# A two-layer graph network: adjacency blocks issued by ScalarE's queue, and four W loads ahead of the residual rows

## The chip, the cores and the metric

The kernel runs on one core of a Trainium2 chip. The time is the device time of that core in microseconds (us). Three runs of the kernel before gave 3094.37, 3098.48 and 3099.01 us; their median is 3098.48 us. The engines are called as in the profile: PE multiplies matrices, DVE does vector work, ACT does activations and copies, POOL (GpSimd) does sums and issues stores, and SP only issues DMAs. Every engine takes its own instructions in order. "SPq" is an instruction that issues a DMA from SP's queue, "ACTq" one from ACT's.

## The reference

There are 2708 rows of 1024 features, and an adjacency matrix of 2708 x 2708 integers, 0 or 1. Two layers follow each other, each with a layer norm ahead and a residual sum behind it:

```python
# layer 0
h = jnp.maximum(_layernorm(x), 0.0)
f = h @ Wf + bf;  g = h @ Wg + bg
e = jax.nn.relu(f @ g.T)
attention = softmax(jnp.where(adj > 0, e, NEG), axis=1)
x = x + attention @ (h @ W + bW)
# layer 1
h = jnp.maximum(_layernorm(x), 0.0)
hw = h @ W1
e = leaky_relu(hw @ a1 + (hw @ a2).T, 0.2)
attention = softmax(jnp.where(adj > 0, e, NEG), axis=1)
x = x + relu(attention @ hw)
```

The scores of layer 0 are a full product of 2708 x 2708 numbers; those of layer 1 are a sum of a column and a row.

## The kernel before

**Panels and pairs.** The scores are made transposed, in five panels p of query columns (576, 576, 532, 512 and 512 wide, `width[p]`). The rows (keys) go in ten pairs q of 128-row tiles, and a rest called LEFT (index 10). Products are taken in Strassen's manner: seven products, named M1 to M7, in the place of eight, and sums by DVE and POOL between them. So `sx`, `sy` and `sz` in the profile are three accumulators of the scores, which take M1 and M2, M5 and M3, M6 and M7 and M4; `px`, `py`, `pz` and `pv` are those of a projection with W.

**Order of the work.** A program for a panel is `project_q` (makes the right operands B), `scores(p, B)`, then softmax and `aggregate` (attention times h), then `project` (times W). `project_q` of the next panel, or in the end `project` of an earlier one, stands between scores and aggregation, so that DVE's softmax lies beside products. The last such projection of the code's layer 0 goes by pairs of tiles (`by_pair`), with the residual rows `x_res` added in `finish0`. It is the one that the change touches, and it runs from about 2085 to 2143 us, ahead of layer 1's aggregation.

**Scores.** For each pair q, `scores` calls `fetch(q + 2)`: the adjacency block of the pair after next, in one stream buffer `adj_i` and, for panels 0 to 2, a slot `adj_t` for the columns over 512. `square_rows` does it by groups of 32 partitions, so a block takes 4 issues and its tail another 4 (8 and 8 for LEFT). Each row's piece is 64 integers of 4 bytes (32 for LEFT). Then come the products M1, M6, M5, M2, M7, M3, and M4, the last one delayed into the next pair. Their left operands `As` come from `hs_d` in DRAM, two products to a tile: M1 with M6, M5 with M2, M7 with M3, and M4 alone. Between the products DVE adds the accumulators into the scores, turns the block of pair q + 1 into a mask (`convert`, `turn`), and does small tasks from a list (`behind`).

**In the first panel** the rows of x are still being read while the scores start: layer norm (`x<-x,rs` on ACT, with its root `rs<-mv`), the transposes `hsT` on PE and ACT, and the stores of `hs_d` for the later pairs run beside the products of the first ones (`make_until(q + 2)`).

**Buffers and queues.** `stream` is a pool of 12 buffers in rotation, for As, adj_i, W (`w`), the left operands of the aggregation (`hc`) and others. A W for one product takes two of them. `load` (L137 to 139) issues from SP and keeps the program's order on the queue. Stores, and the bias that is added into `x_res` in DRAM-to-buffer transfers with an accumulate, are issued by POOL.

**W in the last projection.** `project` loads W for the first two products in `order` (M1 and M5 when by pairs), then calls `start_of`, which for each of the panel's four tiles issues a mask (`maskl`) and the residual rows `x_res` in eight pieces (32 loads in all). W of the other products is loaded where it is used, `ws.pop(m) if m in ws else load_W(l, m)`. By pairs, the whole W is read once for each of the two pairs.

Of the kernel before, what the change touches and what calls it, by code (L numbers as in the profile page):

```python
# [20 lines left out]
B32 = 32  # L21
# [36 lines left out]
def kernel(  # L58
# [19 lines left out]
    nc = InOrder(tc)  # L78
# [46 lines left out]
    def slot(name, shape=(P, WX), dt=FP):  # L125
        return slots.tile(list(shape), dt, tag="slot", name=name)

    def stream(name, shape=(P, D), dt=FP):
        return strm.tile(list(shape), dt, tag="strm", name=name)

    def in_16(o, i):

        n = o.shape[0]
        k = n // 16 * 16
        return [(o, i)] if n in (k, 1) or not k or i.shape[0] != n else [(o[:k], i[:k]), (o[k:], i[k:])]

    def load(o, i):  # L137
        for a, b in in_16(o, i):
            tc.keep_in_program_order(nc.sync.dma_start(a, b))

    def store(o, i):
        for a, b in in_16(o, i):
            nc.gpsimd.dma_start(a, b)  # L143
# [81 lines left out]
    def row_to_all(v, t):  # L225
        load(t, bass.AP(tensor=v.tensor, offset=v.offset, ap=[[0, P], [1, D]]))
        return t
# [38 lines left out]
    def row_on_all(o, row, p, by=load):  # L266
        by(o[:, :width[p]], row[0:1, :width[p]].to_broadcast([P, width[p]]))
# [10 lines left out]
    def load_rows_of(t, o, a):  # L278

        for e in range(2):  # L280
            if t == TINY:
                nc.gpsimd.memset(o[e], 0.0)
            for ps, r in places[t]:
                load(o[e][ps], a[r:r + ps.stop - ps.start, e * W:(e + 1) * W])
# [248 lines left out]
    def fetch_wg(b):  # L533
        return [load_rows(wg, 4 * b + i, "wg") for i in range(4)]
# [60 lines left out]
    ws = fetch_wg(0)  # L595
# [8 lines left out]
    for a in range(NC):  # L604
# [5 lines left out]
        if a == NH:  # L610
# [4 lines left out]
            ws = fetch_wg(1)  # L615
# [150 lines left out]
    def mask_maker(p):  # L766

        r0, w = base[p], width[p]
        NG, NB = P // B32, W // B32
        tail = -(-(w - W) // B32)  # L770
        raw, neg = {}, {}

        def columns(q):

            if q < LEFT:
                return [[start_of_tile(t) + P * g for g in range(NG)] for t in pairs[q]]
            return [[base[g // 2] + W + g % 2 * B32 for g in range(NG)], [base[2] + W] * NG]

        def fetch(q):
            a = stream("adj_i", (P, NB, 2, B32), I32)  # L780
            b = slot("adj_t", (P, tail, 2, B32), I32) if tail else None
            raw[q] = a, b
            c0, c1 = columns(q)

            def square_rows(t, blocks, g, k, r, j, n):
                load(t[B32 * g:B32 * (g + 1), :, k] if k is not None else
                     t[B32 * g:B32 * (g + 1)].rearrange("p b k c -> p b (k c)"),
                     adj[r:r + blocks * B32, j:j + n].rearrange("(b r) j -> r b j", r=B32))
            for t, blocks, r in ((a, NB, r0), (b, tail, r0 + W)):
                for g in range(NG if t is not None else 0):  # L790
                    if q < LEFT:
                        square_rows(t, blocks, g, None, r, c0[g], 2 * B32)
                    else:
                        for k, c in enumerate((c0, c1)):
                            square_rows(t, blocks, g, k, r, c[g], B32)

        def convert(q):
            a, b = raw.pop(q)
            neg[q] = []
            for t, blocks in ((a, NB), (b, tail)):  # L800
                if t is not None:
                    m = slot("nm", (P, 2, blocks, B32), BF)
                    nc.vector.tensor_scalar(m, t.rearrange("p b k c -> p k b c"), 0.0, -BIG, op0=OP.is_le, op1=OP.mult)
                    neg[q].append(m)

        def turn(q, k):
            if k == 0:
                mk_sb[p, q] = slot("mask", (P, 2, WX), BF)
            mk = mk_sb[p, q]
            m = neg[q]  # L810
            nc.vector.transpose(mk[:, k, :W].rearrange("p (s g r) -> p g s r", s=F, g=NG),
                                m[0][:, k].rearrange("p (g s) c -> p g s c", g=NG))
            if tail:
                nc.vector.transpose(mk[:, k, W:W + tail * B32].rearrange("p (b r) -> p b r", r=B32), m[1][:, k])
            if k == 1:
                neg.pop(q)
                store(mk_d[p][:, q], mk[:, :, :w])

        return fetch, convert, turn
# [373 lines left out]
    def load_W(l, m):  # L1193
        ts = [stream("w", (P, 2, W)) for _ in range(2)]
        for g, t in enumerate(ts):
            if m in (M1, M2, M3):
                r, c = (2 * g * P, 0) if m == M1 else ((2 * g + NH) * P, 0 if m == M2 else W)
                load(t, w_in[l][r:r + 2 * P, c:c + W].rearrange("(k p) o -> p k o", p=P))
            else:
                load(t, wt_d[l][:, {M5: 0, M6: 1, M7: 2, M4: 3}[m], 2 * g:2 * g + 2, :])  # L1200
        return [ts[k // 2][:, k % 2] for k in range(NH)]

    def project(l, p, G, finish, then={}, by_pair=False, rate=2.0):
# [10 lines left out]
        start_of, join, finish = finish  # L1214

        order = (M1, M5, M2, M6, M7, M3, M4) if by_pair else (M1, M2, M5, M6, M3, M7, M4)
        ws = {m: load_W(l, m) for m in order[:2]}
        start_of([t for g in todo for t in g[:2]] + ([other] if other else []))
        def left_of(ta, tb, one, two):
            (a11, a12), (a21, a22) = one, two  # L1220
# [33 lines left out]
        for j, group in enumerate([[t] for t in todo] if by_pair else [todo]):  # L1254
            acc, tmp = {}, {}
            left = lefts.pop(j)
            for m in order:
# [4 lines left out]
                for i, (ta, tb, _, _) in enumerate(group):  # L1262
# [9 lines left out]
                    o = {M3: M6, M7: M5, M4: M1}.get(m)  # L1272
# [396 lines left out]
    for p in range(NP):  # L1669
# [8 lines left out]
        if p + 1 < NP:  # L1678
            B = project_q(p + 1, hooks)
        else:  # L1680
            nc.hold = ("vector",)
            project(0, p - 1, G.pop(p - 1), finish0(p - 1), hooks)
            nc.hold = ()
            scores_before()
# [15 lines left out]
        if p < NP - 2:  # L1700
            project(0, p, G.pop(p), finish0(p), {M1: lambda p=p: first_masks(p + 1, 0),
                                                 M5: lambda p=p: first_masks(p + 1, 1),
                                                 M7: lambda p=p: first_masks(p + 1, 2)})
    flush()
    project(0, NP - 1, G.pop(NP - 1), finish0(NP - 1), by_pair=True, rate=0.0)


# [129 lines left out]
```

## Time and profile before

| | us |
|---|---|
| median of three runs | 3098.48 |
| the profiled execution | 3099.78 |
| its span in the profile | 3098.0 |
| PE busy | 3002.8 |
| DVE busy | 2070.7 |
| ACT busy | 463.2 |
| POOL busy | 506.3 |

The granted clock of PE was 0.989 of full speed over the span. In a timeline, a line has the start, the busy time, the engine, the source line, the operation with out and in, and a count of like instructions in a row; in brackets at its end, the idle time ahead of it and what ended that idle time. A line of SPq is a row of DMA issues: its time is the time of the issuing alone, and includes waits between the issues of the row. The chain of waits is followed back from the last instruction; a line "DMA name" in it is the time from an issue to the landing. In the table of windows the columns are the window, its length, then busy time (and count) of PE, PE's weight loads, DVE, ACT and POOL, then the granted clock, the DMA engines' share and GB/s.

The groups that matter for the change, as the profile has them: the scores' products take 293.5 us for `sz`, 199.6 for `sx` and 199.3 for `sy`; before `sx` PE stood idle for 6.4 us in the whole span, before `sz` for 11.8, before `sy` for 2.3.

### The profile page before, as it was taken

To read this page: it belongs to the slowest core of one execution; us is meant where nothing else is said; L and a number is where in the kernel's file an instruction comes from. 1 tells how busy PE (TensorE), PEld (TensorE's weight loads), DVE (VectorE), ACT (ScalarE), POOL (GpSimd) and SP (SyncE) were. 2 spreads that over 40 slices of the span, in tenths; PEclk is the share of its full clock that TensorE was granted. 3 is DMA by queue.
4 is the path that set the end of the run, shared out by engine and by line. 5 is a ranking of instruction groups with operands and counts; after the bars stand their busy time and mean duration, and the time that the engine had idled before them with its cause. 6 is when DMAs were issued, how large, how long until landed. Compare 5 with 4: busy or idle time off the path is not lost.

```text
span 3098.0 us, 41680 instructions
## 1 busy us (share of the span) xinstructions
PE 3002.8 (97%) x14630; PEld 2298.1 (74%) x14630; DVE 2070.7 (67%) x4615; ACT 463.2 (15%) x817; POOL 506.3 (16%) x786
## 2 busy tenths in 40 slices
PE   8998999899999999999999999997999999999998
PEld 4576777657877588885888886783777969879694
DVE  5767693776651596716975277766968768887853
ACT  3420020010110101101011001301222121212200
POOL 1421101310011110214101001141202010020202
PEclk9999999999999999999999999998999999999999
DMA  6999967998565796758967577789667868888896
GB/s 225 291 257 254 301 247 253 309 274 229 178 238 153 217 260 223 244 158 241 278 199 255 164 217 234 237 266 350 229 216 249 274 202 296 287 269 294 264 297 246
DMA packets 448577, 764.70 MB, mean 247 GB/s; under 512 B 175776, under 2 KB 262592, under 8 KB 448368
## 3 DMA queue, kind: packets, MB, share of 16 engines
q1 hardware_dynamic: 393008, 598.31, 62.0%
q0 software_dynamic: 55360, 163.73, 16.4%
q8 instruction: 116, 1.90, 0.3%
q14 instruction: 93, 0.76, 0.1%
HBM read 627.95 MB, written 133.91 MB: 246 GB/s over the span
## 4 chain that ended last, share of the span: by engine, by line
PE 71%; DVE 11%; DMA 7%; issue 7%; SPq 2%; POOL 1%; ACT 1%; POOLq 0%; DVEq 0%; ACTq 0%
PE sz L1378 6%; PE gx L661 6%; PE gy L661 6%; PE gz L661 5%; PE gz L1067 5%; PE pz L1267 4%; PE sx L1378 4%; PE sy L1378 4%; PE px L1267 4%; PE py L1267 3%; PE gx L1067 3%; PE gy L1067 3%; PE M_ps L574 3%; PE qz L661 2%; PE qx L661 2%
## 5 line engine op out<-in xcount | busy, mean ns | idle before, releaser
L1378 PE MATMUL sz<-B,As 128*128 128x288 f32 (+2 forms) x1200 | 293.5, 394 | 11.8 <-DVE st L45 8.8
L1378 PEld LDWEIGHTS sz<-B,As 128*128 128x128 f32 x1200 | 227.8, 191 | 61.8 <-DVE st L45 12.7
L1378 PE MATMUL sx<-B,As 128*128 128x288 f32 (+2 forms) x800 | 199.6, 392 | 6.4 <-DMA As<-hs_d 4.4
L1378 PE MATMUL sy<-B,As 128*128 128x288 f32 (+2 forms) x800 | 199.3, 392 | 2.3 <-DMA As<-hs_d 2.3
L661 PE MATMUL gz<-Sa,hc 128*128 128x288 f32 (+2 forms) x800 | 189.2, 397 | 6.3 <-DMA hc<-hg_d 6.3
L661 PEld LDWEIGHTS gz<-Sa,hc 128*128 128x128 f32 x800 | 153.8, 193 | 40.1 <-DMA hc<-hg_d 6.8
L1378 PEld LDWEIGHTS sx<-B,As 128*128 128x128 f32 x800 | 151.3, 190 | 40.1 <-DMA As<-hs_d 3.7
L1378 PEld LDWEIGHTS sy<-B,As 128*128 128x128 f32 x800 | 152.0, 190 | 33.4 <-issue 2.7
L1067 PE MATMUL gz<-quarter,hc 128*128 128x128 f32 (+2 forms) x1344 | 168.8, 279 | 3.8 <-DVE gT L45 3.7
L143 POOL DMA_DIRECT2D out_dram<-x_res x180 | 89.0, 501 | 482.1 <-DVE x_res L45 474.7
L1067 PEld LDWEIGHTS gz<-quarter,hc 128*128 128x128 f32 x1344 | 160.6, 191 | 5.1 <-DVE gT L45 4.6
L1267 PE MATMUL px<-w,gT 128*128 128x512 f32 x320 | 143.9, 602 | 7.5 <-DMA w<-in_L_gnn_W_dram 6.0
L1267 PE MATMUL pz<-w,ps 128*128 128x512 f32 x320 | 142.1, 594 | 0.8 <-DVE pt L45 0.8
L1267 PE MATMUL py<-w,ps 128*128 128x512 f32 x320 | 142.0, 593 | 0.0
L143 POOL DMA_DIRECT2D mk_d<-mask x55 | 35.8, 652 | 534.8 <-DVE mask L45 528.1
L1267 PEld LDWEIGHTS px<-w,gT 128*128 128x128 f32 x320 | 60.9, 193 | 80.9 <-issue 74.7
L1267 PEld LDWEIGHTS pz<-w,ps 128*128 128x128 f32 x320 | 60.2, 190 | 77.1 <-issue 70.7
L1267 PEld LDWEIGHTS py<-w,ps 128*128 128x128 f32 x320 | 60.5, 190 | 75.8 <-issue 73.9
L574 PE MATMUL M_ps<-wgT,wfT 128*128 128x512 f32 x256 | 113.5, 600 | 1.6 <-ACT hsT L45 1.6
L661 PE MATMUL gy<-T,hc 128*128 128x288 f32 (+2 forms) x480 | 111.6, 394 | 0.0
L977 POOL TENSOR_TENSOR gT<-gT,rr 128x2304 f32<-128x2304 f32 (+5 forms) x12 | 44.4, 3700 | 382.4 <-DVE rr L45 179.8
L661 PEld LDWEIGHTS gy<-T,hc 128*128 128x128 f32 x480 | 91.2, 190 | 19.5
(377 smaller groups left out, 5803.6 us busy)
## 6 DMA issues: line engine op xcount, KB each, us to landing
hc<-hg_d SPq DMA_DIRECT2D x175, 512.0 KB
As<-hs_d SPq DMA_DIRECT2D x150, 512.0 KB
hc<-hr_d SPq DMA_DIRECT2D x119, 512.0 KB
hc<-hs_d SPq DMA_DIRECT2D x112, 512.0 KB
w<-wt_d SPq DMA_DIRECT2D x96, 512.0 KB
w<-in_L_gnn_W_dram SPq DMA_DIRECT2D x72, 512.0 KB
md<-md_d SPq DMA_DIRECT2D x56, 512.0 KB
adj_i<-in_adj_dram SPq DMA_DIRECT2D x200, 128.0 KB
```

What stands on the lines that cost most here:

```text
L143: nc.gpsimd.dma_start(a, b)
L574: nc.tensor.matmul(ps, wfT[a][c // NH][:, c % NH, :], wgT[b][c], start=(c == 0), stop=(c == NC - 1))
L661: nc.tensor.matmul(ps[d], left(m, k, d), right(m, k), start=(start and k == 0), stop=(k == K - 1), skip_group_check=True)
L977: nc.gpsimd.tensor_tensor(of(e, s), of(e, s), by(s, k), OP.mult)
L1067: nc.tensor.matmul(ps[:, d], lhs[:, d * P:(d + 1) * P], inner_right(m, n, k), start=(start and k == 0 and d == 0), stop=(k == NK - 1), ski ...
L1267: nc.tensor.matmul(ps, left[i][m][:, k, :], w_[k], start=(start and k == 0), stop=(k == NH - 1), skip_group_check=True)
L1378: nc.tensor.matmul(ps[:n, :h], lefts[q][:, i % 2, c, :n], B[m][c // 2][:, c % 2, :h], start=(start and c == 0), stop=(c == NH - 1), skip_g ...
```

## The change

First, `load` takes the engine that issues, SP by default. `square_rows` gives ACT for every block from pair 2 on, so that only the first two blocks of a panel stay on SP. This holds for all five panels: in panels 0 to 2, 80 issues each, in panels 3 and 4, 40 each, 320 in all. The blocks, their buffers and their order among themselves stay as they were. Second, `project` loads W for the first four products (M1, M5, M2, M6) ahead of `start_of` when it goes by pairs and `l` is 0, in place of two.

```diff
-    def load(o, i):
+    def load(o, i, by=nc.sync):
         for a, b in in_16(o, i):
-            tc.keep_in_program_order(nc.sync.dma_start(a, b))
+            tc.keep_in_program_order(by.dma_start(a, b))
...
             def square_rows(t, blocks, g, k, r, j, n):
                 load(t[B32 * g:B32 * (g + 1), :, k] if k is not None else
                      t[B32 * g:B32 * (g + 1)].rearrange("p b k c -> p b (k c)"),
-                     adj[r:r + blocks * B32, j:j + n].rearrange("(b r) j -> r b j", r=B32))
+                     adj[r:r + blocks * B32, j:j + n].rearrange("(b r) j -> r b j", r=B32),
+                     nc.scalar if q > 1 else nc.sync)
...
         order = (M1, M5, M2, M6, M7, M3, M4) if by_pair else (M1, M2, M5, M6, M3, M7, M4)
-        ws = {m: load_W(l, m) for m in order[:2]}
+        ws = {m: load_W(l, m) for m in order[:4 if by_pair and l == 0 else 2]}
         start_of([t for g in todo for t in g[:2]] + ([other] if other else []))
```

## The prediction

> **What bounds the kernel now.** I read the page's busy table first, then the chain of waits, then the DMA issues, and then TensorE's timeline, looking for bracketed idle times in the stages that the change touches.
>
> ```profile
> PE 3002.8 (97%) x14630; PEld 2298.1 (74%) x14630; DVE 2070.7 (67%) x4615; ACT 463.2 (15%) x817; POOL 506.3 (16%) x786
> ...
> PE 71%; DVE 11%; DMA 7%; issue 7%; SPq 2%; POOL 1%; ACT 1%; POOLq 0%; DVEq 0%; ACTq 0%
> ...
> As<-hs_d SPq DMA_DIRECT2D x150, 512.0 KB
> ...
> adj_i<-in_adj_dram SPq DMA_DIRECT2D x200, 128.0 KB
> ```
>
> TensorE (PE) works for 3002.8 of 3098.0 us: 95.2 us of idle time is all that better feeding could ever give, and a delay counts in full as soon as it reaches PE. ACT is busy for 15%, so issuing there looks free; but its queue is in order, and what stands behind an issue matters, not its share. As (the left operands of the scores, 512 KB each) and the adjacency blocks both come from SP's queue. In the first panel's scores (about 218 to 375 us) PE waits for As:
>
> ```profile
> 224.24 2.11 PE L1378 MATMUL sy<-B,As 128*128 128x288 f32 x8
> ...
> 246.00 3.63 PE L1378 MATMUL sz<-B,As 128*128 128x288 f32 x8 [2.38 <-DMA As<-hs_d]
> ...
> 253.94 2.21 PE L1378 MATMUL sx<-B,As 128*128 128x288 f32 x8 [2.13 <-DMA As<-hs_d]
> ...
> 278.58 2.18 PE L1378 MATMUL sy<-B,As 128*128 128x288 f32 x8 [2.25 <-DMA As<-hs_d]
> ```
>
> With 0.70 at 270.24 and 1.57 at 288.14 these five waits make 9.03 us: the whole that part A can win there. SP's timeline shows what As stands behind:
>
> ```profile
> 198.25 2.23 SPq L139 DMA_DIRECT2D adj_i<-in_adj_dram  x4
> ...
> 203.00 11.70 SPq L139 DMA_DIRECT2D x<-in_x_dram  x16
> 214.80 0.94 SPq L139 DMA_DIRECT2D As<-hs_d  x2
> 215.91 3.74 SPq L139 DMA_DIRECT2D adj_i<-in_adj_dram  x4
> ...
> 271.78 11.47 SPq L139 DMA_DIRECT2D adj_t<-in_adj_dram  x4
> 284.24 2.17 SPq L139 DMA_DIRECT2D As<-hs_d  x4
> ```
>
> The chain of waits gives the reason at 271.78: an issue waits for the landing of an earlier adjacency block.
>
> ```profile
> 262.31 6.14 DMA adj_t<-in_adj_dram
> ...
> 268.51 15.65 DMA adj_i<-in_adj_dram
> ```
>
> **What the skill says.** The Trainium skill, "DMA: Bandwidth & Descriptors", section "Issuing engines are not separate DMA queues", says that DMAs of SP, ACT and POOL run on the same 16 engines, and that a second issuer saves only the issuing time. The trace agrees as far as it goes: at 200 to 300 us the DMA share is 0.91 to 1.04, so there is no idle transfer capacity for a second queue to use. [...] "Perfetto Trace Analysis", section "DMA Instruction — HWDGE (DVE, Sync)", says that the record of an issue leaves out the transfer; I therefore take landings from the chain (3.85 us the shortest adjacency landing, at 1457.50; As 3.77 and 6.98).
>
> **What the built programs add.** In both, every DMA issued by SP or ACT signals one of eight shared semaphores, and each waits until the DMA before it on its semaphore has landed. The order across the two queues is thus fixed: at most eight are under way, and an SP load can wait for a block that ACT has not issued yet. The move does not free As from adj; it makes SP's loads depend on how far ACT is.
>
> **Part A, first scores.** Removed from SP: 80 issues (8 for each of eight row pairs, 16 for the rest). Added to ACT: the same 80. ACT's timeline shows where they come to stand:
>
> ```profile
> 220.13 1.52 ACT L45 ACTIVATE x<-x,rs 128x512 f32<-128x512 f32 x2 [1.02 <-DVE rs L45]
> ...
> 238.00 1.52 ACT L45 ACTIVATE x<-x,rs 128x512 f32<-128x512 f32 x2 [0.48 <-DVE rs L45]
> 242.18 0.30 ACT L45 ACTIVATE rs<-mv,eps 128x1 f32<-128x1 f32 x1 [2.66 <-DVE mv L45]
> ```
>
> (1) Pair 2's blocks, which SP issued at 198.25 to 202.4, follow the x copies of 220.13 on ACT, so most start at 221.7 or later. In SP's queue the second to ninth of the 16 x loads wait for these blocks' semaphores, and behind the x loads stands the As tile for M5 and M2 of pair 0 (214.80 before). First landing 221.7 + 3.85 = 225.6. The x loads took 11.70 us for 16; at half to two thirds of that As is issued at 231 to 233 and lands 3.8 to 7 later, 235 to 240. PE needs it at 224.24: a stall of 11 to 15, of which I take 12. Nothing hides it, since PE has no other product ready.
> (2) After such a pause PE is slower: after the pauses of 8.33 and 3.85 us before 2160 the granted clock was 0.70.
>
> ```profile
> 2150.00:2175.00 25.00, 19.51 (x70) 14.34 (x71) 25.00 (x65) 9.26 (x17) 2.90 (x4) 0.70 0.78 243
> ```
>
> The first gx group there took 21.60 us, the next 19.40; I take +1.5 (0 to 2).
> (3) Pair 3's eight issues follow the x copies of 238.00 and stand ahead of the root of 242.18 and the hsT copies of 244.38; the sixth waits until the first has landed. DVE's reciprocal after that root is in DVE's in-order queue, behind it the addition that PE's M7 waits for. +3 to +8; I take +4.
> (4) The five waits of 9.03: PE comes 12 us later, so its As tiles are there, but the transfers that SP couldn't start are also late, in a stage whose transfers are full. I take -7 (-9 to 0).
> Sum of the first scores: 12 + 1.5 + 4 - 7 = +10.5.
>
> **Part A, later scores.** Panel 1: pair 2's blocks go from 630.73 on SP to after 661.12 on ACT; As for M1 and M6 of pair 1 then waits for their landing near 669, lands 674 to 676, needed at 672.83: +2 to +3. Pair 3's follow the x_res copies of 678.84, and As of pair 2 comes about 3 us late, partly beside waits for DVE that are there anyway. I take +3.5 (0 to 6). Panels 2 and 3: the same step leaves As of pair 1 at 1099 (needed 1099.4) and 1465 (needed 1464.2): +1.5 together (0 to 4). Panel 4: ACT is free and PE doesn't wait for loads: 0.
>
> **Part B.** Before, only W for M1 and M5 stands ahead of 32 x_res loads and four masks; M2's comes after them:
>
> ```profile
> 2080.83 7.90 SPq L139 DMA_DIRECT2D x_res<-in_x_dram  x8
> 2088.77 1.82 SPq L139 DMA_DIRECT2D w<-in_L_gnn_W_dram  x2
> ...
> 2098.14 6.29 PE L1267 MATMUL px<-w,gT 128*128 128x512 f32 x8 [5.96 <-DMA w<-in_L_gnn_W_dram]
> ```
>
> Moved up: four issues, 2 MB. They go, but need four stream buffers that the aggregation frees between 2060.3 and 2068.6, so x_res starts near 2069 instead of 2058.97. The 5.96 go, perhaps 0.78 at the next product as well: -6.7 at most. Next late is W for M7 (issued at 2090.69 before), behind the same x_res loads at about 2099, 1 to 5 us; and DVE's first sum with x_res (2092.21), which already waited 2.45 us for the bias. I take -3 (-6 to +2).
>
> **Sum.** 10.5 + 3.5 + 1.5 - 3 = +12.5. The profiled execution has 3099.78 us (span 3098.0, 1.78 outside it), the median of the three runs is 3098.48; on the median this is 3111.0.
>
> **Rivals.**
> - As freed (faster). If ACT's blocks are issued early enough, before about 220, the M5 tile isn't late; As no longer stands behind 11 us of adjacency issues, all 9.03 go and part B gives 3: 3098.5 - 12 = 3086.5. For it: the five brackets and 271.78. Against it: the shared semaphores, and ACT's x copies at 220.13.
> - Given back (no change). The stall of 12 comes, with its 1.5, but scores that start later find all their loads there (-9) and part B gives -5: about 3098. For it: most loads after 250 wait for buffers that PE frees. Against it: the full DMA engines.
> - ACT blocked everywhere (heavier). The upper ends: 15 + 1.5 + 8 - 7, then 6, 4 and 2: +29.5, 3128. For it: each ACT block can wait for its own landings. Against it: ACT has little to do after 260.55.
>
> **How the numbers follow.** Forecast 0.50, faster 0.20, given back 0.18, heavier 0.12. Range 3088 to 3126: it leaves out about half of the faster case and half of the heavier, 0.16. Without the faster case the forecast's own range is 3104 to 3120. What a measurement can tell from no change is 0.2%, 6.2 us: faster 0.21 (the faster case and an edge of "given back"), same 0.19, slower 0.60.
>
> **What would show it.** In the changed kernel's trace: x loads on SP pausing from 203 to about 225; one wait of 10 us or more for As at the first sy products; less than 3 us of As waits from 246 to 290; ACT's roots behind adjacency issues; As waits of 2 to 3 us near 672 on top of the shift; no W wait at px, a smaller one at the M7 pz. I am wrong if SP's x loads go on at 204, or if the M5 tile lands before PE asks for it.

## The result, and the profile after

The changed kernel took 3117.49 us (median of six runs, 3114.05 to 3122.06); the kernel before, run beside it, 3097.6 us. The ratio is 1.0065, with a 95% interval of 1.0052 to 1.0078: about 20 us slower, where +12.5 was forecast. The profiled execution took 3114.05 us, the shortest of the six, so that what is found in it (+14.3 against the first profile of before) falls short of the whole.

The first lines of the two parts of the page, engines and chain of waits, of the changed kernel:

```profile
PE 3002.5 (96%) x14630; PEld 2299.3 (74%) x14630; DVE 2070.3 (67%) x4615; ACT 463.1 (15%) x817; POOL 506.1 (16%) x786
...
PE 69%; DVE 9%; issue 7%; DMA 5%; POOL 1%; ACT 1%; SPq 0%; ACTq 0%; POOLq 0%; DVEq 0%
```

PE is busy for the same time (3002.5 against 3002.8 us), so in sum what was lost is time in which PE waits: 109.7 us of the span of 3112.2, against 95.2. SP's timeline at the start of the first scores, the place where the prediction put the loss:

```profile
193.40 0.38 SPq L139 DMA_DIRECT2D As<-hs_d  x1
194.88 28.92 SPq L139 DMA_DIRECT2D x<-in_x_dram  x16
223.90 1.33 SPq L139 DMA_DIRECT2D As<-hs_d  x3
```

The 16 x loads that took 11.70 us before take 28.92, and As stands behind them. The view of waits, for SP from 190 to 225 us (total, times, longest), names what they wait for:

```profile
SPq L139 <- DMA adj_i<-in_adj_dram: 21.3, 3, 20.1
```

One wait of 20.1 us is for an adjacency block, which is no longer in SP's queue. ACT's timeline has it:

```profile
211.06 0.29 ACT L45 ACTIVATE rs<-mv,eps 128x1 f32<-128x1 f32 x1 [7.15 <-DVE mv L45]
211.17 0.38 ACTq L45 DMA_DIRECT2D adj_i<-in_adj_dram  x1
...
212.48 0.81 ACT L45 ACTIVATE x<-x,rs 128x512 f32<-128x512 f32 x1 [1.02 <-DVE rs L45]
...
214.07 1.99 ACTq L45 DMA_DIRECT2D adj_t<-in_adj_dram  x4
```

The first of the block's eight issues goes out at 211.17, right behind a root of the layer norm for which ACT had waited 7.15 us (for DVE's `mv`), and SP's next x load at 215.27. PE's timeline, lines with an idle time ahead of them and one that follows such a line:

```profile
227.88 4.18 PE L1379 MATMUL sy<-B,As 128*128 128x288 f32 x8 [11.13 <-DMA As<-hs_d]
231.85 3.14 PE L1379 MATMUL sx<-B,As 128*128 128x288 f32 x8
...
258.28 3.65 PE L1379 MATMUL sz<-B,As 128*128 128x288 f32 x8 [7.96 <-DVE st L45]
...
290.79 3.04 PE L1379 MATMUL sy<-B,As 128*128 128x288 f32 x8 [3.38 <-DMA As<-hs_d]
```

There are two new waits, 11.13 us for As at the first `sy` (M5 of pair 0) and 7.96 us for DVE at M7 of pair 1. The groups behind the first are slow (4.18 and 3.14 us in place of 2.10). The windows of this stretch have the clock in the third column from the end:

```profile
220.00:230.00 10.00, 2.12 (x5) 1.57 (x6) 0.00 (x0) 0.00 (x0) 0.00 (x0) 0.51 0.87 287
230.00:240.00 10.00, 10.00 (x35) 7.54 (x34) 6.92 (x18) 0.00 (x0) 1.30 (x2) 0.80 0.24 85
```

The chain of waits shows how the second wait comes about:

```profile
244.95 8.83 DMA adj_i<-in_adj_dram
...
255.18 2.05 ACT hsT L45 x4
257.23 0.20 ACT rs L45
257.45 0.17 DVE rs L45
...
257.78 0.46 DVE st L45
258.24 0.04 issue
258.28 3.65 PE sz L1379 x8
```

One of pair 3's eight issues on ACT waits for the landing of the first (8.83 us). Behind the eight stand the copies hsT and the root; behind the root, in DVE's queue, the reciprocal and then the sum `st`, which M7 needs.

In the last projection, SP's timeline of the changed kernel, and PE's:

```profile
2102.53 5.54 SPq L139 DMA_DIRECT2D x_res<-in_x_dram  x8
2108.17 1.19 SPq L139 DMA_DIRECT2D w<-wt_d  x2
2109.45 0.90 SPq L139 DMA_DIRECT2D w<-in_L_gnn_W_dram  x2
```

```profile
2119.86 2.04 PE L1268 MATMUL py<-w,ps 128*128 128x512 f32 x2 [11.05 <-DMA w<-in_L_gnn_W_dram]
```

The wait of 5.96 us at M2 is gone, and one of 11.05 stands at M3, whose W (the last of the three lines of SP) is issued behind all residual rows.

For the experiments, this table has the length of some stages, from the first product of a stage to the first of the next, read from PE's timelines (us):

| profile | first scores begin | first scores | scores 1 | scores 2 | scores 3 | last aggregation | last projection |
|---|---|---|---|---|---|---|---|
| before | 218.5 | 164.1 | 151.9 | 138.7 | 137.8 | 133.6 | 75.8 |
| before, again | 210.7 | 170.9 | 149.5 | 138.7 | 137.7 | 133.9 | 75.1 |
| changed | 210.9 | 183.9 | 150.2 | 140.3 | 136.0 | 134.5 | 79.7 |
| A alone | 209.2 | 185.3 | 150.3 | 141.5 | 136.0 | 133.7 | 75.0 |
| A, pair 2 early | 210.6 | 176.5 | 150.2 | 140.1 | 136.0 | 133.5 | 75.8 |
| A from pair 3 | 215.9 | 172.3 | 152.7 | 141.1 | 138.2 | 133.4 | 75.7 |
| A from pair 4 | 208.8 | 162.9 | 149.6 | 141.7 | 137.7 | 133.7 | 75.3 |
| B alone | 209.2 | 164.9 | 149.6 | 138.7 | 137.5 | 136.3 | 76.9 |
| A, pair 2 early, pair 3 on SP | 210.6 | 171.8 | 149.6 | 141.6 | 136.0 | 134.1 | 75.5 |
| A, first panel on SP | 220.8 | 165.2 | 152.4 | 141.7 | 136.0 | 133.9 | 74.9 |
| first panel from pair 4 | 211.6 | 164.5 | 150.7 | 138.6 | 137.8 | 133.9 | 75.7 |

### The profile page after: what moved, and what is told of

Read it like the earlier page. It is cut to its first block, busy times and chain, and to the rows that moved or that the text cites. A ratio compares the mean times of both kernels' runs of the same rounds, so it can differ in the third digit from the quotient of the medians.

```text
span 3112.2 us, 41664 instructions
## 1 busy us (share of the span) xinstructions
PE 3002.5 (96%) x14630; PEld 2299.3 (74%) x14630; DVE 2070.3 (67%) x4615; ACT 463.1 (15%) x817; POOL 506.1 (16%) x786
## 4 chain that ended last, share of the span: by engine, by line
PE 69%; DVE 9%; issue 7%; DMA 5%; POOL 1%; ACT 1%; SPq 0%; ACTq 0%; POOLq 0%; DVEq 0%
PE sz L1379 6%; PE gx L661 6%; PE gy L661 6%; PE gz L661 5%; PE gz L1068 5%; PE sy L1379 4%; PE sx L1379 4%; PE px L1268 4%; PE pz L1268 4%; PE py L1268 3%; PE gy L1068 3%; PE gx L1068 3%; PE gv L661 3%; PE qz L661 2%; PE qx L661 2%
## 5 line engine op out<-in xcount | busy, mean ns | idle before, releaser
L1379 PE MATMUL sz<-B,As 128*128 128x288 f32 (+2 forms) x1200 | 293.4, 394 | 15.9 <-DVE st L45 14.3
```

The lines of the kernel that those rows point to most:

```text
L1379: nc.tensor.matmul(ps[:n, :h], lefts[q][:, i % 2, c, :n], B[m][c // 2][:, c % 2, :h], start=(start and c == 0), stop=(c == NH - 1), skip_g ...
```

## The experiments

All were timed against the kernel before, except the second look at it. A ratio is followed by its 95% interval. A ratio of 1.001 is 3.1 us. The edits are shown against the changed kernel; in those that follow part B alone, W is loaded as before the change, unless the edit says otherwise.

**The two parts apart.** Part A alone leaves W as before:

```diff
-        ws = {m: load_W(l, m) for m in order[:4 if by_pair and l == 0 else 2]}
+        ws = {m: load_W(l, m) for m in order[:2]}
```

> Part A alone: all adjacency blocks from pair 2 on issued by ACT, W as before (two products ahead). The trace of the changed kernel puts some 4 us of its 20 on part B (the residual rows come late, W for M4 waits), so the theory that both parts cost expects before + 14 to + 17 us, about 3113, with the waits at the first sy (11 us, for As) and at M7 of pair 1 (8 us, for DVE) unchanged. If part B were a gain, as the prediction had it (-3), this kernel would be slower than the changed one: above 3118.

Measured: 1.0052 [1.0036, 1.0067], about +16 us. The waits at the first sy and at M7 are 11.97 and 8.02 us. Part B alone gives all blocks back to SP:

```diff
-                     nc.scalar if q > 1 else nc.sync)
+                     nc.sync)
```

> Part B alone: all blocks on SP, W for four products ahead of the residual rows by pairs. Theory from the changed kernel's trace: the wait of 6 us at px goes and a wait of about 11 us for W comes four products later, before + 3 to + 5 us: 3101 to 3103. The prediction had -3: about 3095.

Measured: 1.0013 [1.0005, 1.0021], about +4 us. The sum of both, +20, is the whole change's. So about four fifths of the loss are part A's, and part B is a small loss (its interval is 1.5 to 6.5 us) and not the gain that was forecast. PE's timeline of part B alone:

```profile
2052.49 16.00 PE L661 MATMUL gv<-Sb,hc 128*128 128x256 f32 x64 [2.03 <-DVE m L45]
...
2096.53 2.04 PE L1268 MATMUL py<-w,ps 128*128 128x512 f32 x2 [8.28 <-DMA w<-in_L_gnn_W_dram]
```

**A second look at the kernel before.**

> The kernel before once more, unchanged, for a second profile. In the first profile PE waited 4.35 us for DVE at 190 us, ahead of the first scores, which none of the changed kernels' profiles has; it comes from the landing time of the first two adjacency blocks, which no part of the change touches. If this is chance, a second profile may start the first scores near 209 to 211 us, as the others do; the first scores themselves should take about 164 us up to the next panel's products, as in the first profile.

Measured: one time, 3097.99 us. The first scores begin at 210.69, so the 4.35 us at 190 us in the first profile were chance. But the expected 164 us were missed: the stage took 170.92, with these waits on PE:

```profile
249.01 4.00 PE L1378 MATMUL sx<-B,As 128*128 128x288 f32 x8 [9.33 <-DMA As<-hs_d]
284.08 4.18 PE L1378 MATMUL sx<-B,As 128*128 128x288 f32 x8 [4.10 <-DMA As<-hs_d]
```

In this profile the scores begin early, and waits for As take the gain back. That is not the rule: B alone, with the same loads in this panel, began at 209.2 and took 164.9 us. Six profiles here have the first panel's blocks all on SP; three of them took 164.1 to 165.2 us in this stage and three 170.2 to 170.9, and neither group goes with an early or a late start. So single profiles of this stage differ by some 6 us, for a reason that wasn't found; only the timed ratios size it.

**Position or queue: pair 2's block earlier on ACT.** `fetch(2)` of the first panel moves from the head of the scores into the projection before:

```diff
             turn(0, 0)
             turn(0, 1)
+            if p == 0:
+                fetch(2)
...
-            if q + 2 <= LEFT:
+            if q + 2 <= LEFT and (p or q):
                 fetch(q + 2)
```

> Part A alone, but in the first panel pair 2's block is fetched earlier in the program, so that its eight issues stand on ACT ahead of the roots and x copies of the last rows and not behind them. Theory of position (SP's x loads and the As tile behind them wait for blocks that ACT issues late): the wait of 11 us at the first sy goes, the one at M7 of pair 1 (pair 3's block) stays, so before + 3 to + 8 us, 3101 to 3106. Rival (two hardware queues share the DMA engines by packets, and small adjacency packets slow the As loads wherever they are issued): no change from part A alone, about 3113.

Measured: 1.0041 [1.0027, 1.0055], +13 us: a miss, between the two and nearer to the rival by time. The trace says which part of each is so (two lines of PE's timeline, then two of ACT's):

```profile
221.01 3.70 PE L1381 MATMUL sy<-B,As 128*128 128x288 f32 x8 [4.55 <-DMA As<-hs_d]
250.69 4.21 PE L1381 MATMUL sz<-B,As 128*128 128x288 f32 x8 [8.54 <-DVE st L45]
```

```profile
195.15 1.56 ACT L45 COPY hsT<-h_ps 128x512 f32<-128x512 f32 x3 [18.21 <-PE h_ps L443]
196.52 0.38 ACTq L45 DMA_DIRECT2D adj_i<-in_adj_dram  x1
```

The first wait falls from 11.97 to 4.55, not to nothing; the second stays in full. The block is not as early as was meant: it now stands behind hsT copies for which ACT had waited 18.21 us (for PE), and SP's 16 x loads of that moment take 17.80 us, 8.9 of them in a wait for an adjacency block, against 7.53 in the changed kernel. By time alone this run decides little, since the intervals of the two kernels overlap.

**Pair 2's block back on SP.**

```diff
-                     nc.scalar if q > 1 else nc.sync)
+                     nc.scalar if q > 2 else nc.sync)
```

> Part A from pair 3 on: only pair 2's block goes back to SP. Theory of position with two separate waits: the wait of 11 us for As at the first sy goes, the one of 8 us at M7 of pair 1 stays (pair 3's eight issues still stand ahead of the root on ACT), so before + 6 to + 12 us, 3102 to 3108. If the second wait were only a consequence of the first (all loads late), it would go as well: before - 3 to + 2.

Measured: 1.0031 [1.0023, 1.0039], +10 us, as the theory of two separate waits has it. PE's timeline:

```profile
221.66 2.11 PE L1379 MATMUL sy<-B,As 128*128 128x288 f32 x8
...
251.21 3.88 PE L1379 MATMUL sz<-B,As 128*128 128x288 f32 x8 [10.17 <-DVE st L45]
```

The wait at the first sy (221.66) is gone, with no bracket there; that at M7 is there without it.

**Pairs 2 and 3 back on SP** (`q > 3` in the same line).

> Part A from pair 4 on only: pairs 2 and 3 stay on SP, 64 of the first panel's 80 issues are still ACT's, and none of them stands ahead of a root of the layer norm. Theory of position: both new waits go, and some of the 9 us of As waits of before with them: before - 7 to + 1 us, 3091 to 3099. Rival (sharing by packets): four fifths of the cost of part A remain, about 3110.

Measured: 0.9995 [0.9986, 1.0004]. With 64 of the first panel's 80 issues still ACT's, the whole loss is gone. The rival, as it was put (four fifths of the cost remain), is out.

**Both edits: pair 2 early on ACT, pair 3 on SP.**

```diff
-                     nc.scalar if q > 1 else nc.sync)
+                     nc.scalar if q > 1 and q != 3 else nc.sync)
```

> Part A alone with both edits at once: pair 2's block on ACT but fetched ahead of the roots and x copies (72 of the first panel's 80 issues are ACT's), pair 3's back on SP. Theory of position: neither the wait at the first sy (11 us; 4.5 were left of it with the early block alone) nor the one at M7 of pair 1 (8 to 10 us) is there, before - 3 to + 5 us. Rival (ACT's queue itself is the cost in the first panel): about before + 14, as for part A alone.

Measured: 1.0007 [0.9998, 1.0016], +2 us. Now 72 of 80 issues are ACT's, pair 2's among them, and 14 of 16 us are gone. What costs is where an issue stands in ACT's queue, not that it is ACT's. The time is as expected, one wait is not: the one at M7 is gone, but the first `sy` still waits 5.44 us for As, with the block behind the same hsT copies as in the run with pair 2 early. A later wait for As is 6.26. Before's second profile has such waits of 9.33 and 4.10, and the whole stage took 171.8 and 170.9 us, so that the 5.44 us don't show in the time.

**The first panel's blocks all on SP, the other four panels' on ACT** (`q > 1 and p > 0`).

> Part A in panels 1 to 4 only, the first panel's blocks all on SP. The prediction had + 5 us for these panels (3.5 and 1.5). From the changed kernel's trace, panels 1 to 4 together are within - 2 to + 1 us: before - 2 to + 1, 3094 to 3097. A cost of ACT's queue as such would show here as well, at 240 of 320 issues: + 8 or more.

Measured: 1.0003 [0.9994, 1.0013]. So 240 of the 320 moved issues cost 1 us or so, 4 at the most. The table shows what it is made of: scores 2 are 1.4 to 3.1 us longer wherever ACT issues their blocks, with new waits for As of 0.2 to 1.8 us each; scores 3 are 1.8 us shorter wherever pair 2's block is ACT's. Why those are shorter wasn't tried: a wait of 1.37 us for DVE's `sm` at M2 of the first pair is gone.

**Can the last projection be mended?** First, W for M2 and M6 between the residual rows of the two pairs of tiles:

```diff
-        start_of([t for g in todo for t in g[:2]] + ([other] if other else []))
+        if by_pair and l == 0:
+            start_of(todo[0][:2])
+            ws.update({m: load_W(l, m) for m in order[2:4]})
+            start_of(todo[1][:2])
+        else:
+            start_of([t for g in todo for t in g[:2]] + ([other] if other else []))
```

> Only the last projection is changed, all blocks on SP: W for M1 and M5 first, then the residual rows of the first pair of tiles, then W for M2 and M6, then the residual rows of the second pair. If part B fails because the residual rows stand behind four W at once and W for M7 and M3 behind them, this gives the wait at px (5.96 us) back without a wait of the same size later: before - 3 to - 6 us, 3090 to 3093. If the loads are bounded by the DMA engines' rate alone (share 0.94 to 1.04 there), the wait only moves: within 1 us of before.

Measured: 1.0003 [0.9995, 1.0011]: about 1 us slower than before (3.4 at the most), as the rival said, and no gain of 3 to 6. The wait at px is gone and there is one of 6.98 us at M3:

```profile
2111.46 2.05 PE L1273 MATMUL py<-w,ps 128*128 128x512 f32 x2 [6.98 <-DMA w<-in_L_gnn_W_dram]
```

Next, `order[2:6]` in the place of `order[2:4]`: W for M2, M6, M7 and M3 between.

> Only the last projection: W for M1 and M5, the residual rows of the first pair of tiles, then W for M2, M6, M7 and M3, then the residual rows of the second pair. With W for M2 and M6 only put between, the wait at px went and one of 7 us at M3's first products came: W for M7 and M3 stood behind the second pair's residual rows. Theory of order: with those behind, no wait of over 2 us stays in the projection, before - 3 to - 6 us. Rival of rate (the same bytes are needed in the same time whatever their order): some other load waits in its place, within 1.5 us of before.

Measured: 1.0018 [1.0009, 1.0026], +5.6 us. Both theories missed: it is slower, and by more than the 1.5 us that the rival allowed. Two lines of PE's timeline, and a window with the clock, the DMA share and GB/s at its end:

```profile
2102.82 5.40 PE L1273 MATMUL pz<-w,ps 128*128 128x512 f32 x8 [2.34 <-DVE pt L45]
...
2132.53 5.46 PE L1273 MATMUL pz<-w,ps 128*128 128x512 f32 x6 [5.77 <-DMA w<-wt_d]
```

```profile
2075.00:2100.00 25.00, 25.00 (x89) 15.20 (x87) 12.24 (x21) 0.59 (x1) 10.22 (x11) 1.00 1.05 339
```

Until 2099 PE has no wait in the projection. Then it waits for DVE, which had itself stood idle 7.40 us for the bias transfer into the first pair's residual rows (12.61 us from issue to landing in the chain of waits). In the second pair W is late; its issue at 2112.32 takes 20.07 us to land. The idle times make 12.5 us in all, against 6.7 before. The share of the DMA engines is 1.05 up to 2100 us, and 0.91 in the next 25 us, in which the second pair waits. The bytes are the same in each order, and each order that was tried moved the waits to other work. With three orders that all failed to gain, the projection's 6 us look like a matter of rate. That is argued and not shown: a version with fewer bytes there wasn't tried, and rate alone doesn't say why this order is worse than the others.

**A version that gains.** ACT issues the first panel's blocks from pair 4 on, and nothing else:

```diff
-                     nc.scalar if q > 1 else nc.sync)
+                     nc.scalar if p == 0 and q > 3 else nc.sync)
```

> ACT issues the blocks from pair 4 on in the first panel only, all other panels as before. With all panels from pair 4 on the time was before - 1.5 us, with panel 2 some 3 us longer and the first panel 1 us shorter in the profile. Expected: before - 1 to - 5 us. If the first panel's gain in that profile was chance, within 1 us of before.

Measured: 0.9987 [0.9980, 0.9995], about -4 us (between -6 and -1.5): faster than both kernels, at the edge of what can be told. The profiles fit without settling it: with these blocks on ACT, the first scores took 162.9, 164.5 and 163.6 us in three profiles, and none has the 170 us of half of the profiles with all blocks on SP. With the projection's last order (W for four products between) on top:

> The two mended parts together: blocks of the first panel from pair 4 on by ACT, and W and residual rows of the last projection in the order of the kernel before this one. If both gain, the sum: before - 4 to - 11 us. If loads are bounded by rate in both places: within 2 us of before.

Measured: 1.0007 [0.9997, 1.0016]. The projection's loss (5.67 us of waiting for W at a later `pz` again) takes the gain back.

## Why the prediction was right or wrong

The direction and the range were right: slower, 3117.49 in 3088 to 3126. The forecast's sum was some 7 us short, and its terms were off in both directions: some 5 us too little in the first scores, 4 too much in the later ones, 7 too little for part B. That the sum came as near as it did owes something to chance.

**The first scores, +10.5.** The mechanism was right. Step (1) took 12 for the As tile behind the x loads: 11.13 measured, for the reason given, with SP waiting 20.1 us for a block of ACT's. The kernel with pair 2 on SP confirms it, the wait being gone. (That it is the shared completions which tie the two queues was read from the built programs, and the 20.1 us fit it; a kernel without the sharing wasn't tried.) Two errors partly cancel inside the step. The first issue came ahead of the x copies, not behind them, so that SP went on some 2.7 us earlier than forecast (its stage began 7.65 us earlier in this profile); and the x loads then took 8.6 us up to As, where half to two thirds of 11.70 were reckoned, 5.9 to 7.8. Step (2) took 1.5 for the clock: sy and sx behind the wait are 2.08 and 1.04 us longer, so 3.1, and the window has 0.51. (The group of 19.40 us that the step compares with is a `gy` group, and 19.40 is its distance to the next; its busy time is 19.56.) Step (3) is the term that was mis-sized: +4 taken, 3 to 8 given. The wait at M7 was 7.96, 8.54 and 10.17 us in three kernels, at the upper end of what was given or beyond it; where it stands alone, with pair 3 on ACT and pair 2 not, the time is +10 us. The eight issues do not only take their time: the later ones wait for the landing of the first (8.83), and then the hsT copies (2.05) go ahead of the root. Step (4) took -7 of the 9.03 us: 3.81 us of As waits and 1.45 of a DVE wait were left, so some -4 to -5. So part A cost about the 15.5 us of its whole sum, but nearly all of it in this panel, where 10.5 were put.

**The later scores, +5.** Wrong: the four later panels together cost about 1 us. In panel 1 the wait of 2 to 3 us at pair 1 didn't come. One at pair 2 did (2.26 us at 699.74), but the waits for DVE that stand there in before (0.57 and 0.73) went, so that the stage is within 2 us of both profiles of before. The lateness was added to those waits nearly in full, and it partly lies in their place. In panel 2 the size of 1.5 was about right, but not the place: the wait is at 1140.90, more than 30 us later in the stage than pair 1, at which it was put. In panel 3 there was a gain, where none was given.

**Part B, -3.** Wrong in sign, and outside its own -6 to +2: +4. The step that failed is "Next late is W for M7 ..., 1 to 5 us". The wait moved to the first products of M3, which stand ahead of M7's, and grew to 8.28 us (B alone) and 11.05 (changed kernel), since W for both stands behind 32 loads of residual rows that themselves start later: 11.8 us ahead of the projection's first product in B alone, 26.2 us before, where the prediction reckoned with some 16. The prediction used the share of the DMA engines for the first scores (against "given back") and not here, where it is 0.94 to 1.04 from 2050 to 2125 us in the first profile. In B alone the aggregation ahead is 2.7 us longer as well, with a slow `gv` behind a wait of 2.03 us. How much of that is chance stays open: the two kernels with W between have the same SP order up to W for M6, and took 135.97 us (with a slow `gv` too) and 133.45 us in that stage.

**The rivals.** "As freed" needed ACT's blocks early: with pair 2 early and pair 3 on SP it gave +2 us and no gain. "Given back" was half right for As. "ACT blocked everywhere" was right about the first panel's second wait alone. The statement that "the move does not free As from adj" held; what could be gained by moving blocks, from pair 4 on, was 4 us.

## What to carry to other kernels

Before issuing loads from an engine that looks idle, find what it does at the very place. An issue behind an instruction that waits for another engine (here a root that waits for DVE, or copies that wait for PE) is late. Where it waits for a landing itself, the work behind it is late too, and with it whatever needs that work. Where completions are shared between two queues, a late issue in one can hold the other, as SP was held for 20.1 us here. And where a stage's DMA share is already about 1, as in the projection here, expect that a load moved ahead moves the wait to a load that it passes; count the bytes before the order.

## What was not expected

Two executions of one program differ by several microseconds at 190 us, long before anything that the change touches: the wait for DVE's `m` was between 0 and 6.74 us in the profiles here, and the first scores began between 208.8 and 220.8. The two profiles of before begin 7.8 us apart there and end 1.8 us apart, since waits for As take the early start back in one of them; in B alone's profile they don't, and nothing here says which it will be.

The Trainium skill, "TensorE: Matmul & The Clock Gate", section "What's actually happening", gives half clock after at least one idle window of about 3.4 us. The 11.13 us wait agrees: 0.51 in its window. But shorter waits did it too. In B alone a wait of 2.03 us ahead of `gv` was followed by 16.00 us in place of 14.32 for the same 64 products, with a granted clock of 0.68 from 2052 to 2057 us. In the kernel with W for two products between, a wait of 1.67 us was followed by 16.00 us as well. In the changed kernel, a wait of 1.91 us at the same place left 14.32, and the clock was 1.00 from 2074.7 to 2079.7 us:

```profile
2074.74 14.32 PE L661 MATMUL gv<-Sb,hc 128*128 128x256 f32 x64 [1.91 <-DVE m L45]
```

So a short wait can cost nearly its own length again, or nothing, and its length alone doesn't say which.
